# Seven seldom needed expert blocks as one loop behind one branch, in a Mamba and mixture-of-experts kernel

## Chip, core and metric

The kernel runs on one core of one Trainium2 chip. The metric is the device time of one execution in microseconds (us), the median of three runs. Engines are named as in the profile: PE (matrix products; PEld is its weight load), DVE (vector), ACT (scalar), POOL (GpSimd, which here issues the indirect DMAs) and SP (SyncE, which issues the plain DMAs).

## The reference

An input of 4096 tokens of width 256 goes through a state-space (Mamba) layer and then through a layer of eight experts, each with a residual and a LayerNorm behind it. A token is given to one expert alone, the one with the largest logit.

```python
def _L0_ffn_ref(x, Wr, br, W1, b1, W2, b2):
    D_MODEL, D_FF, N_EXP = (256, 1024, 8)
    xf = x.reshape(-1, D)
    logits = xf @ Wr.T + br
    expert_idx = jnp.argmax(logits, axis=-1)
    h = jax.nn.relu(jnp.einsum('td,efd->etf', xf, W1) + b1[:, None, :])
    y = jnp.einsum('etf,edf->etd', h, W2) + b2[:, None, :]
    out = y[expert_idx, jnp.arange(xf.shape[0])]
    return out.reshape(B, S, D)

x = L0_attn_input_tensor                      # (1, 4096, 256), float32
x = _layernorm(x + _L0_attn_ref(x, ...))      # the Mamba layer
x = _layernorm(x + _L0_ffn_ref(x, ...))       # the expert layer
```

## The kernel before

The Mamba layer works in eight blocks of 512 tokens. As soon as enough tokens have passed it, the kernel sorts them by expert and gathers them into expert blocks of 128 rows; every block has one expert. Because experts can end in blocks that are not full, up to `NSB` = 39 blocks can be needed. The first `SURE` = 32 are always computed; blocks 32 to 38, the **seldom blocks**, are needed only where the tokens are spread unluckily. A count on the chip, `total`, is loaded into a register of every engine (`held[1]`, line 1128), and a branch (`tc.If`, line 656) skips seldom blocks that are not needed. In this input none is needed: no product of a seldom block is in the trace.

**One expert block**, in the order in which PE works:

- `turn(b)` transposes the gathered rows `xg` (line 553), and DVE copies the result to `xgT` (line 564). It is issued one block ahead.
- `hidden(b, half)` makes half of the 1024 hidden columns (line 581): 16 of the 32 recorded products of a block for each half. ACT adds the bias and clips the first half (line 590), DVE the second (line 592); the result is `hT`.
- `close(b, half)` multiplies `hT` by the second weights into the accumulator `pe` (line 606).
- `finish(b)` adds up on DVE: `xs` = `xg` + b2 (line 629), `r` = `pe` + `xs` (line 631), then `layernorm` (lines 254 to 261, with one square root on ACT, line 259), which leaves `y`.
- `scatter(b)` sends `y` to its rows of the output by an indirect DMA on POOL (line 645).

Blocks 17, 20, 23, 26 and 29 are `LONG`: they hold 32 or 64 rows more, their hidden rows lie in a wider buffer (`wide`), the products of the extra rows come behind the others (line 617), and a second LayerNorm follows.

**Weights.** A block's expert weights are 128 rows of 4360 float32 values, 2.2 MB. Three buffers, `held_weights`, hold them: block b uses buffer b modulo 3. `prefetch(b)` (lines 508 to 524) gathers rows and weights up to two blocks ahead, through POOL. Where the block three before has the same expert, the load is suppressed by an index out of bounds; `same` in `table` says so, and it is set to zero where a seldom block may have overwritten the buffer.

**Order.** PE's order is the order of the program (`manual_schedule`). For the other engines a scheduler chooses the order, but nothing moves across a branch. The generator `blocks()` runs blocks 0 to 31; the first ones lie beside the Mamba layer, the last ones alone. After a block that stands in `SELDOM`, `seldom(after)` issues one branch with one or two seldom blocks in it. There are four branches: behind blocks 27 (two seldom blocks), 28 (two), 29 (one) and 31 (two). The first three follow the whole `finish` of their block. The last one precedes the `finish` of block 31. The rows of the seldom blocks are gathered into one buffer during blocks 22 to 26 (`gather_seldom`), are replaced there by the results where a block is computed, and are scattered during blocks 29 to 31 and at the end. Where the block is not needed, the indices of its scatter are out of bounds.

Of the kernel before, what the change touches and what calls it, by code (L numbers as in the profile page):

```python
# [37 lines left out]
F32 = mybir.dt.float32  # L38
# [4 lines left out]
ALU = mybir.AluOpType  # L43
# [4 lines left out]
P = 128  # L48
T, D = 4096, 256
# [30 lines left out]


SELDOM = {SURE - 5: (0, 1), SURE - 4: (2, 3), SURE - 3: (4,), SURE - 1: (5, 6)}
EPS = 1e-5
# [17 lines left out]
def mamba_moe(  # L101
# [173 lines left out]
    def order(b0, b):  # L275

        if b0 == EARLY[6] and b < SURE - b0:
            b = b % SLOTS * RUN + b // SLOTS
        return slice(b, b + 1)

    def table(b0, nb, columns, rows, early):
# [131 lines left out]
        if not early:  # L413
# [9 lines left out]

            for b in SELDOM:
                if b + SLOTS < SURE:
                    nc.vector.memset(same[:, order(b0, b + SLOTS - b0)], 0.0)
            nc.vector.scalar_tensor_tensor(eb, same, float(NE * P), eb, ALU.mult, ALU.add)
# [70 lines left out]

    xgf, openf, yf, ends_, wide_, seldom_in = {}, {}, {}, {}, {}, []
    current = 0  # L500
# [35 lines left out]
    def seldom_rows():  # L536
# [4 lines left out]
        return seldom_in[0]  # L541

    def gather_seldom(b):
        xgs[b] = ys[b] = seldom_rows()[:, (b - SURE) * D : (b - SURE + 1) * D]
        gather(xgs[b], *index[b])

# [49 lines left out]
    def close(b, half):  # L596
# [15 lines left out]
        if b in LONG:  # L612

            openf[b], n = bank("o", f"pf{b}"), more_of(b)
            for fc in range(FC):
# [4 lines left out]
                )  # L620
        if b != SURE - 1:
            finish(b)

    def finish(b):
        xg, we, py = xgs[b], wes[b], open_[b]
        xs = m2.tile([P, D], F32, tag="xs", name=f"xs{b}")

        with tc.issue_after(last[b].ins):
            nc.vector.tensor_tensor(xs, xg, we[:, OC : OC + D], ALU.add)
        r = m2.tile([P, D], F32, tag="r", name=f"r{b}")  # L630
        nc.vector.tensor_tensor(r, py[:, 0:D], xs, ALU.add)  # L631
        if b < SURE:
            ys[b] = m2.tile([P, D], F32, tag="y", name=f"y{b}")
        layernorm(m2, r, ys[b], f"m{b}")
# [17 lines left out]

    def seldom(after):

        first = SURE + SELDOM[after][0]
        with tc.If(held[1] > (first - EARLY[6]) * P, preferred_fallthrough_block=False):  # L656
            for b in (SURE + n for n in SELDOM[after]):
                wes[b] = held_weights[(after if after < SURE - 1 else after - 1) % SLOTS]
                row = nc.values_load(
                    spare[0:1, b - SURE : b - SURE + 1], engines=[mybir.EngineType.SP],  # L660
                    min_val=0, max_val=(NE - 1) * P,
                )
                nc.sync.dma_start(wes[b], experts[bass.ds(row, P), :])
                turn(b)
                for half in range(2):
                    hidden(b, half)
                for half in range(2):
                    close(b, half)

    def blocks():  # L670

        nonlocal current
        for b in range(SURE):
            current = b
            if b - 1 in SELDOM:
                seldom(b - 1)
            prefetch(b)

            for n in SELDOM.get(b + 5, ()):
                gather_seldom(SURE + n)  # L680

            if 0 < b:
                scatter(b - 1)
            for n in SELDOM.get(b - 2, ()):
                scatter(SURE + n)
            if b not in turned:
# [439 lines left out]
    for _ in quarters:  # L1126
        if current == min(SELDOM) - 3 and len(held) == 1:
            held += nc.values_load_multi_w_load_instructions(
                held[0], min_val=0, max_val=NSB * P, bass_reorder=False
            )[1]  # L1130

    seldom(SURE - 1)
    for n in SELDOM[SURE - 1]:
        scatter(SURE + n)
    finish(SURE - 1)
    scatter(SURE - 1)

# [43 lines left out]
```

## Time and profile before

| what | value |
|---|---|
| median of three runs | 494.23 us (493.94 to 494.93) |
| the profiled execution | 493.76 us |
| its span, first to last instruction | 492.1 us |
| granted PE clock, mean over the span | 0.991 |
| busy: PE, PEld, DVE, ACT, POOL | 472.7, 353.0, 346.9, 218.8, 187.3 us |
| PE's last product ends | 484.17 us |

A span is counted from the first instruction on the core to the last; the time of an execution has some 1.7 us more around it. In the profile a row of a timeline gives the start, the busy time, the engine, the line, the operation, the tiles (output, then inputs), the shapes and the number of merged instructions; in brackets stands how long the engine was idle before it and what released it. "DVEq" is the instruction queue of DVE: branches and semaphore steps, which don't count as work. Matmuls are pipelined, so their rows overlap a little, and their ends are modelled.

### The profile page before, as it was taken

The numbers are of one execution on the slowest core, as the hardware profiler recorded it, in microseconds if no ns is written. First come the engines' busy times: TensorE is split into PE (matmuls) and PEld (weight loads), VectorE is DVE, ScalarE is ACT, GpSimd is POOL, SyncE is SP. The second block draws the span as 40 slices with busy tenths as digits, with TensorE's granted clock in tenths as the row PEclk, the third lists the DMA queues.
The fourth block names the chain that finished last, engine by engine and source line by source line (L and its number), as shares of the span: only waits on it lengthen the run. The fifth ranks groups of instructions, "written<-read, shape, count | busy, mean of one in ns | idle before, by whom it ended". The sixth has DMA issues, their size and how long they took to land. (4 is left out here: it accounts for less than half of the span.)

```text
span 492.1 us, 7641 instructions
## 1 busy us (share of the span) xinstructions
PE 472.7 (96%) x2602; PEld 353.0 (72%) x2602; DVE 346.9 (71%) x1161; ACT 218.8 (44%) x452; POOL 187.3 (38%) x193
## 2 busy tenths in 40 slices
PE   8999999999999999999999999999999999998893
PEld 5344645555464675777889998999989898987782
DVE  2587979797999889869899788545565655453352
ACT  4786778777878774845342221221212121211120
POOL 2002122444447345233415242444444466542433
PEclk9999999999999999999999999999999999998997
DMA  8401012120308908506666587999871599486500
GB/s 235 156 1 44 0 44 85 45 85 1 128 1 349 361 18 277 191 2 224 218 259 254 214 296 263 375 346 367 325 300 50 202 321 318 143 293 254 194 17 23
DMA packets 23052, 89.59 MB, mean 182 GB/s; under 512 B 4898, under 2 KB 14629, under 8 KB 19298
## 3 DMA queue, kind: packets, MB, share of 16 engines
q0 software_dynamic: 8672, 74.29, 41.3%
q1 hardware_dynamic: 13378, 14.50, 9.1%
q8 instruction: 23, 0.38, 0.3%
q10 hardware_dynamic: 960, 0.27, 0.3%
q14 instruction: 19, 0.16, 0.1%
HBM read 87.35 MB, written 9.54 MB: 197 GB/s over the span
## 5 line engine op out<-in xcount | busy, mean ns | idle before, releaser
L722 PE MATMUL pm<-xTb,win 128*128 128x512 f32 (+1 forms) x260 | 120.6, 595 | 0.5 <-DMA win<-in_W_in 0.5
L581 PEld LDWEIGHTS ph<-xgT,we 128*128 128x128 f32 x864 | 102.2, 194 | 9.7 <-DVEq L656 2.7
L581 PE MATMUL ph<-xgT,we 128*128 128x128 f32 x864 | 104.9, 279 | 3.3 <-DMA out<-long,tidx 2.3
L606 PE MATMUL pe<-we,hT 128*128 128x256 f32 x432 | 99.9, 381 | 0.7 <-DVE hT L592 0.7
L606 PEld LDWEIGHTS pe<-we,hT 128*128 128x128 f32 x432 | 79.5, 190 | 11.7 <-DVE hT L592 1.5
L735 DVE SCALAR_TENSOR_TENSOR acc<-xc,cw,acc 128x512 f32<-128x512 f32 x96 | 71.2, 771 | 15.5 <-ACT acc L731 15.1
L722 PEld LDWEIGHTS pm<-xTb,win 128*128 128x128 f32 x260 | 47.3, 191 | 46.9 <-issue 40.4
L520 POOL DMA_INDIRECT we<-in_experts,widx x32 | 33.8, 1056 | 95.6 <-DVE r L631 32.3
L259 ACT ACTIVATE sdm<-sdm 128x1 f32<-128x1 f32 x32 | 6.5, 202 | 132.8 <-DVE sdm L258 132.7
L890 PE MATMUL po<-wout,sg 128*128 128x264 f32 x256 | 64.1, 392 | 0.0
L854 POOL TENSOR_TENSOR sg<-cv,sg 128x512 f32<-128x512 f32 x22 | 33.9, 1543 | 59.2 <-DVE cv L849 44.3
L890 PEld LDWEIGHTS po<-wout,sg 128*128 128x128 f32 x256 | 46.0, 190 | 10.2 <-issue 2.9
L592 DVE TENSOR_SCALAR hT<-ph,we 128x128 f32<-128x128 f32 x108 | 31.5, 343 | 29.4 <-issue 9.7
L645 POOL DMA_INDIRECT out<-y,tidx x32 | 32.9, 1028 | 42.2 <-DVE y L261 30.0
L503 POOL DMA_INDIRECT xg<-x1d,tidx x32 | 32.3, 1010 | 31.7 <-issue 6.6
L631 DVE TENSOR_TENSOR r<-pe,xs 128x256 f32<-128x256 f32 x32 | 13.5, 422 | 42.3 <-PE pe L606 38.5
L590 ACT ACTIVATE hT<-ph,we 128x128 f32<-128x128 f32 x108 | 30.8, 366 | 26.5 <-PE ph L581 18.3
L979 POOL TENSOR_SCALAR rowh<-lrow,row,code 128x256 f16<-128x256 bf16 x20 | 25.8, 1299 | 26.8 <-DVE row L971 26.8
L849 DVE SCALAR_TENSOR_TENSOR cv<-cv,dp,py 128x256 f32<-128x256 f32 x64 | 28.9, 470 | 2.4 <-PE py L842 2.4
L727 ACT ACTIVATE sg<-pm 128x512 f32<-128x512 f32 x32 | 19.0, 595 | 17.1 <-PE pm L722 14.8
L581 PE MATMUL ph<-wide,we 128*128 128x160 f32 (+1 forms) x160 | 24.4, 310 | 2.3 <-DVEq L656 2.3
L581 PEld LDWEIGHTS ph<-wide,we 128*128 128x128 f32 x160 | 23.8, 190 | 2.9 <-DVEq L656 2.7
(221 smaller groups left out, 612.3 us busy)
## 6 DMA issues: line engine op xcount, KB each, us to landing
xb<-in_x SPq DMA_DIRECT2D x8, 512.0 KB, 4.8
x1d<-x SPq DMA_DIRECT2D x8, 512.0 KB, 5.4
xTb<-in_xT SPq DMA_DIRECT2D x7, 512.0 KB, 3.5
win<-in_W_in SPq DMA_DIRECT2D x1, 512.0 KB
we<-in_W_outT SPq DMA_DIRECT2D x1, 512.0 KB
wout<-in_W_out SPq DMA_DIRECT2D x1, 512.0 KB
we<-in_experts,widx POOLq DMA_INDIRECT x32
xg<-x1d,tidx POOLq DMA_INDIRECT x32
```

What stands on the lines that cost most here:

```text
L503: nc.gpsimd.indirect_dma_start(out=to, out_offset=None, in_=x1d[0:rows, :], in_offset=bass.IndirectOffsetOnAxis(ap=at, axis=0),)
L520: nc.gpsimd.indirect_dma_start(out=wes[n][:, :], out_offset=None, in_=experts, in_offset=bass.IndirectOffsetOnAxis(ap=weights[n], axis=0), ...
L581: nc.tensor.matmul(ph[:, n * w : (n + 1) * w], lhsT=we[:, at : at + P], rhs=xgT[:, dc * w : (dc + 1) * w], start=(dc == 0), stop=(dc == DC ...
L590: nc.scalar.activation(hT[:, fc, :], ph[:, n * w : (n + 1) * w], AF.Relu, bias=bias)
L592: last[b] = nc.vector.tensor_scalar(hT[:, fc, :], ph[:, n * w : (n + 1) * w], bias, 0.0, ALU.add, ALU.max)
L606: nc.tensor.matmul(py[:, 0:D], lhsT=hT[:, fc, 0:P], rhs=out_weights(fc), start=(fc == 0), stop=(fc == FC - 1),)
L645: moved = nc.gpsimd.indirect_dma_start(out=out, out_offset=bass.IndirectOffsetOnAxis(ap=at, axis=0), in_=rows, in_offset=None, bounds_chec ...
L722: nc.tensor.matmul(pm[:, at], lhsT=win[:, dc, c * P : (c + 1) * P], rhs=xTb[:, dc, at], start=(dc == 0), stop=(dc == DC - 1),)
L735: nc.vector.scalar_tensor_tensor(acc, xc[:, c, k : k + TB], cw[:, c, k : k + 1], acc, ALU.mult, ALU.add)
L849: nc.vector.scalar_tensor_tensor(cv[:, c, at], cv[:, c, at], dp[:, c : c + 1], py[:, 0 : TB // 2], ALU.mult, ALU.add,)
L854: eng.tensor_tensor(sg[:, c, :], cv[:, c, :], sg[:, c, :], ALU.mult)
L890: nc.tensor.matmul(po[:, 0 : D + NE], lhsT=sg[:, c, j * P : (j + 1) * P], rhs=wout[:, c, :], start=(c == 0), stop=(c == CC - 1),)
```

## The change

Four branches with one or two seldom blocks each become one branch, behind the products of block 28. Inside it a loop of seven rounds (`tc.For_i`) computes one seldom block in each round: it loads the expert's weights and the block's rows by SP's queue, computes, and stores the result in place of the rows. The `finish` of block 28 comes after the branch. `xs` = `xg` + b2 moves from `finish` to the end of `close`, for every block, so that for block 28 it is ahead of the branch. The gathers of the seldom rows lie in blocks 22 to 25 and their scatters in blocks 30 and 31. One weight load (block 31's) is forced where there were two (blocks 30 and 31), and the count is loaded into the registers in block 25 rather than in block 24.

```diff
-SELDOM = {SURE - 5: (0, 1), SURE - 4: (2, 3), SURE - 3: (4,), SURE - 1: (5, 6)}
+SELDOM = SURE - 4
...
-            for b in SELDOM:
-                if b + SLOTS < SURE:
-                    nc.vector.memset(same[:, order(b0, b + SLOTS - b0)], 0.0)
+            nc.vector.memset(same[:, order(b0, SELDOM + SLOTS - b0)], 0.0)
...
-    def gather_seldom(b):
-        xgs[b] = ys[b] = seldom_rows()[:, (b - SURE) * D : (b - SURE + 1) * D]
-        gather(xgs[b], *index[b])
...
-        if b != SURE - 1:
+        xss[b] = m2.tile([P, D], F32, tag="xs", name=f"xs{b}")
+
+        with tc.issue_after(last[b].ins):
+            nc.vector.tensor_tensor(xss[b], xgs[b], we[:, OC : OC + D], ALU.add)
+        if b != SELDOM:
             finish(b)
 
     def finish(b):
-        xg, we, py = xgs[b], wes[b], open_[b]
-        xs = m2.tile([P, D], F32, tag="xs", name=f"xs{b}")
-
-        with tc.issue_after(last[b].ins):
-            nc.vector.tensor_tensor(xs, xg, we[:, OC : OC + D], ALU.add)
+        we, py, xs = wes[b], open_[b], xss[b]
         r = m2.tile([P, D], F32, tag="r", name=f"r{b}")
         nc.vector.tensor_tensor(r, py[:, 0:D], xs, ALU.add)
-        if b < SURE:
-            ys[b] = m2.tile([P, D], F32, tag="y", name=f"y{b}")
+        ys[b] = m2.tile([P, D], F32, tag="y", name=f"y{b}")
         layernorm(m2, r, ys[b], f"m{b}")
...
-    def seldom(after):
-
-        first = SURE + SELDOM[after][0]
-        with tc.If(held[1] > (first - EARLY[6]) * P, preferred_fallthrough_block=False):
-            for b in (SURE + n for n in SELDOM[after]):
-                wes[b] = held_weights[(after if after < SURE - 1 else after - 1) % SLOTS]
+    def seldom():
+
+        with tc.If(held[1] > (SURE - EARLY[6]) * P, preferred_fallthrough_block=False):
+            with tc.For_i(0, NSB - SURE) as n:
+                b = SURE
+                at = seldom_rows()[:, bass.ds(n * D, D)]
+                wes[b] = held_weights[SELDOM % SLOTS]
                 row = nc.values_load(
-                    spare[0:1, b - SURE : b - SURE + 1], engines=[mybir.EngineType.SP],
+                    spare[0:1, bass.ds(n, 1)], engines=[mybir.EngineType.SP],
                     min_val=0, max_val=(NE - 1) * P,
                 )
                 nc.sync.dma_start(wes[b], experts[bass.ds(row, P), :])
+                one = m2.tile([P, D], F32, tag="y", name="seldom_x")
+                nc.sync.dma_start(one, at)
+                xgs[b] = one
                 turn(b)
                 for half in range(2):
                     hidden(b, half)
                 for half in range(2):
                     close(b, half)
+                nc.sync.dma_start(at, ys[b])
 
     def blocks():
...
-            if b - 1 in SELDOM:
-                seldom(b - 1)
+            if b - 1 == SELDOM:
+                seldom()
+                finish(SELDOM)
             prefetch(b)
 
-            for n in SELDOM.get(b + 5, ()):
-                gather_seldom(SURE + n)
+            if SELDOM - 6 <= b < SELDOM - 2:
+                for n in range(SURE + b - SELDOM + 6, NSB, 4):
+                    gather(seldom_rows()[:, (n - SURE) * D : (n - SURE + 1) * D], *index[n])
 
             if 0 < b:
                 scatter(b - 1)
-            for n in SELDOM.get(b - 2, ()):
-                scatter(SURE + n)
+            for n in range(b + 2, NSB, 2) if b >= SURE - 2 else ():
+                ys[n] = seldom_rows()[:, (n - SURE) * D : (n - SURE + 1) * D]
+                scatter(n)
...
-        if current == min(SELDOM) - 3 and len(held) == 1:
+        if current == SELDOM - 3 and len(held) == 1:
...
-    seldom(SURE - 1)
-    for n in SELDOM[SURE - 1]:
-        scatter(SURE + n)
-    finish(SURE - 1)
     scatter(SURE - 1)
```

More of the change, by code (lines that the diff above doesn't have):

```diff
@@ L496, in mamba_moe @@
     xgs, wes, turned, hid, last, open_, ys = {}, {}, {}, {}, {}, {}, {}
-    xgf, openf, yf, ends_, wide_, seldom_in = {}, {}, {}, {}, {}, []
+    xgf, openf, yf, ends_, wide_, xss, seldom_in = {}, {}, {}, {}, {}, {}, []
     current = 0
```

## The prediction

> **What bounds the kernel now.** I read the page first, then TensorE's timeline from 434 us on, the instructions of line 656 (the `If`), the stage table, and last the timeline of all engines in the tail.
>
> ```profile
> PE 472.7 (96%) x2602; PEld 353.0 (72%) x2602; DVE 346.9 (71%) x1161; ACT 218.8 (44%) x452; POOL 187.3 (38%) x193
> ...
> PEclk9999999999999999999999999999999999998997
> ```
>
> PE works 96% of the span, so only what stops PE, or lies behind its last product, is worth time. The clock row has one low slice before the end (an 8, at 443 to 455 us). The timeline shows why both matter here:
>
> ```profile
> 435.32 3.84 PE L581 MATMUL ph<-xgT,we 128*128 128x128 f32 x32
> 439.00 0.38 PE L553 MATMUL pg<-ident,xg 128*128 128x128 f32 x2
> 439.22 3.62 PE L606 MATMUL pe<-we,hT 128*128 128x256 f32 x16
> 445.16 5.47 PE L581 MATMUL ph<-xgT,we 128*128 128x128 f32 x32 [2.33 <-DMA out<-long,tidx]
> ...
> 457.38 5.47 PE L581 MATMUL ph<-wide,we 128*128 128x192 f32 x32 [2.32 <-DVEq L656]
> ...
> 469.04 3.81 PE L581 MATMUL ph<-xgT,we 128*128 128x128 f32 x32 [0.65 <-DVE y L261]
> ```
>
> The first three lines are block 27. Blocks 28, 29 and 30 start at 445.16, 457.38 and 469.04, each just after a branch (behind blocks 27, 28 and 29), and PE stands still before them for 2.33, 2.32 and 0.65 us. The only other PE gap above 0.25 us after 415 us is 0.35 us inside block 30. The DMA named at 445.16 had nothing to give; the wait is the next line's, DVE's branch:
>
> ```profile
> 456.85 0.41 DVE L261 TENSOR_SCALAR y<-r,mvm,sdm 128x256 f32<-128x256 f32 x1
> ...
> 457.38 5.17 PEld L581 LDWEIGHTS ph<-wide,we 128*128 128x128 f32 x32 [2.73 <-DVEq L656]
> ```
>
> `y` of block 28 ends at 457.26, DVE's semaphore step of line 656 falls at 457.30, PE loads weights at 457.38. So each engine that jumps over the block first waits for its own work to end, then adds to its counter what the skipped body would have added; PE's next product waits for DVE's addition, and DVE stands behind a whole LayerNorm.
>
> ```profile
> 442.80:445.10 2.30, 0.04 (x1) 0.00 (x0) 1.77 (x6) 0.20 (x1) 0.00 (x0) 1.00 0.69 266
> 445.10:450.50 5.40, 5.34 (x33) 5.34 (x33) 0.00 (x0) 1.14 (x4) 3.02 (x3) 0.68 0.58 195
> 455.00:457.30 2.30, 0.05 (x1) 0.00 (x0) 1.76 (x6) 0.20 (x1) 0.00 (x0) 1.00 0.04 12
> ```
>
> Stage rows give length, busy time of PE, PEld, DVE, ACT, POOL, then clock, DMA share, GB/s. In the two stalls DVE alone works (1.77 us of LayerNorm). After the first one the clock is 0.68 of full, and 32 products that took 3.84 us in block 27 take 5.47 us.
>
> [...]the clock is 0.5 from 445.70 to 449.11, 3.41 us[...] 2.33 us of idleness lay in the 3.41 us before. The second stall, of equal length, [...]costs nothing more. [...]PE's second branch instruction takes 0.28 to 0.31 us in all four places[...]. [...]here it is 34 to 55 ns on four engines, 64 to 310 ns on PE.[...]
>
> **The change, part by part.**
>
> *Branch behind block 27 gone.* Block 28 can start when 27 ends, as block 27 did behind 26 (no gap at 435.3). Its weights landed by 436.9, its `xgT` was copied at 440.89. Gain 2.33 us. Without this idleness [...]the half clock goes too: 5.47 - 3.84 = 1.63 us. Bounds for that: 0 (if the timed executions have no such window[...]) to twice that (if both stalls fell so); I take 1.63.
>
> *Branch behind block 29 gone.* Gain 0.65 us. Block 29 has a second group of products (L617, 1.95 us) behind the first, so DVE's `y` was nearly done when PE came; what remained is PE's own passage: products end at 468.39, own semaphore step at 468.45, branch at 468.60 for 0.28, one more wait step at 468.94, weights at 469.01. This is my price for a branch on PE alone.
>
> *Branch behind block 28 stays, ahead of `r` and the LayerNorm.* DVE's last work before it is then `xs` (it ended near 452.7, 2.4 us ahead of PE's last product), so DVE and ACT add to their counters while PE still multiplies. PE pays its own passage: 2.32 - 0.65 = 1.67 us gained. Bounds of what is left: 0.3 us (the branch instruction alone) to 3.4 us (the join below). Late next: nothing. The LayerNorm (2.2 us from `r` to the end of `y`) now runs beside block 29's first products, whose DVE half comes only about 2.7 us after its start (half of 5.47); if it slips, some tenths on `hT`.
>
> *`xs` moved up.* One 0.41 us DVE addition per block, already issued before the branch behind 27, 28 and 29 (at 452.24 for block 28). Nothing.
>
> *The loop body.* Skipped: no product of it is in the trace, and the test is that of the first branch before. Its seven row loads and seven stores on SP's queue are skipped too; SP passed its four branches at 297.6 to 299.5 and has no work behind them until the end. Nothing.
>
> *POOL.* Seven gathers and seven scatters stay, at 1.28 us each (0.97 busy and 0.30 between); two gathers move from block 26 into 24 and 25. They can delay a weight load by 1.3 us; the load for 29, issued at 436.19, landed at 446.33, and block 29 would start at 451.7, so 5 us cover it. Block 30 need no longer reload its weights by force; that load (446.01 to 455.60) was 13 us early, so nothing. The load for 31 stands behind the branch and behind block 28's products, as before; it took 9.7 us (458.19 to 467.88) and has about 18. The scatters are now four in block 30 and three in block 31: `y` of block 30 and three take 5.1 us of the 7.0 us until the last `y`. Covered; each one past that costs 1.28.
>
> *Register loads* (0.49 to 0.56 us an engine) move one block later; PE's, at 409.30, stood beside products with no gap. *One memset* less on DVE near 298 us. Nothing.
>
> *The tail.* 484.17 to 492.1, 7.9 us:
>
> ```profile
> 485.96 0.41 DVE L261 TENSOR_SCALAR y<-r,mvm,sdm 128x256 f32<-128x256 f32 x1
> 488.20 0.98 POOL L645 DMA_INDIRECT out<-y,tidx  x1 [3.74 <-issue]
> ```
>
> The last scatter starts 1.83 us behind its `y`; for block 30 it was 0.28 us (479.35 to 479.63). The last branch had long been passed by POOL (479.5), so I can't tie the extra 1.55 us to it: bounds 1.55 gained to 1.55 lost (the same delay once more behind the four scatters before it), value 0. The 0.35 us inside block 30 likewise stays.
>
> **The sum** on the profiled execution: 2.33 + 1.63 + 1.67 + 0.65 = 6.28 us. PE would end near 477.9 and the span be 485.8 instead of 492.1; the execution's own time of 493.76 becomes 487.5. The median of the three runs is 494.23, 0.47 above it; taken from the median: **487.9 us**.
>
> **Rivals.**
>
> 1. *The clock part does not show* (no half-clock window in the timed executions, or one after the remaining branch): gain 4.65, time 489.6.[...] Against: 493.76 with such a window lies close to all three runs.
>
> 2. *The branch becomes a join.* If a loop in the skipped body makes the skipping path meet on all engines and empty the DMA queues, PE waits for what is in flight at 451: the forward weight load (issued at 443, 9.6 us) and a scatter behind it, to about 453, and two meetings like the program's end (491.27 to 492.03, 0.76 us). About 2.7 us more: 490.6, and 492.2 if that idleness halves the clock. Against: no branch of before shows a meeting.
>
> 3. *It doesn't do what it says*: `r` and LayerNorm still stand ahead of the branch on DVE. Then 2.32 stays: gain 4.61, time 489.6. The order of the code speaks against it.
>
> 4. *Slower: block 31's weights come late.* POOL's order is a scheduler's, and it now orders all after the branch at once. The load takes 9.7 us and block 31 would start at 470.7, so it hurts if issued after 461.0 and makes the kernel slower if issued after about 468.3. That needs it behind block 29's scatters (ready near 465) and the four seldom ones (5.1 us): issued at 470, landed at 480, 9.3 us of stall and 1.6 of half clock, so 499. Against: before, the load (458.19) went ahead of even block 28's scatter (459.51).
>
> **How the numbers follow.** Forecast 0.64, rival 1 0.14, rival 2 0.09, rival 3 0.06, rival 4 and its like 0.07. The range goes from 485.9 (forecast with the tail's 1.55 and the 0.35) to 491.2 (rivals 1 and 3 with a tail 1.6 longer, rival 2 at its likelier end). About 0.2%, 1 us, is what a measurement can tell from no change. Faster 0.90, within 0.03, slower 0.07.
>
> **What would show it.** In the profile after: one PE gap of some 0.65 us after block 28 and none after 27 and 29; block 28's 32 products in about 3.8 us with no low clock slice before the end; `xs` of 28 before and `r` behind DVE's only branch; seven scatters of seldom rows ahead of the last `y`; PE ending near 478. Wrong if the remaining gap exceeds 2 us, or a new gap stands before block 30 or 31.

## The result and the profile after

| what | before | after |
|---|---|---|
| median of four runs each, on one chip | 494.58 us (493.94 to 495.44) | 487.7 us (486.77 to 488.9) |
| ratio of the times | | 0.9862 [0.9836, 0.9888] |
| the profiled execution | 493.76 us | 486.77 us |
| its span | 492.1 us | 485.0 us |
| PE's last product ends | 484.17 us | 477.13 us |

The changed kernel is faster by 6.9 us, where 6.3 were forecast. Its 487.7 us lie closer to the forecast of 487.9 than the two gains do, in part because the kernel before, timed again beside it, took 0.35 us longer than in the first three runs (494.58 for 494.23). PE's busy time falls by 1.7 us (472.7 to 471.0), the others change by 1.1 us at most, and the clock row has lost its low slice in front of the last one:

```profile
PE 471.0 (97%) x2602; PEld 351.9 (73%) x2602; DVE 346.9 (72%) x1160; ACT 218.8 (45%) x452; POOL 186.9 (39%) x193
...
PEclk9999999999999999999999999999999999999998
```

The same work is done with less standing about. PE's timeline shows where (start, busy time, engine, line, operation, tiles, shapes, instructions; in brackets the idle time before it and what ended it). In this kernel L574 is `hidden`, L599 `close`, L624 the addition `r`, L260 the `y` of the LayerNorm, L617 `xs`, L637 the scatter and L647 the branch:

```profile
439.39 3.62 PE L599 MATMUL pe<-we,hT 128*128 128x256 f32 x16
442.85 3.73 PE L574 MATMUL ph<-xgT,we 128*128 128x128 f32 x32
...
451.67 5.44 PE L574 MATMUL ph<-wide,we 128*128 128x192 f32 x32 [0.66 <-DVE r L624]
...
462.59 3.84 PE L574 MATMUL ph<-xgT,we 128*128 128x128 f32 x32
...
473.51 3.62 PE L599 MATMUL pe<-we,hT 128*128 128x256 f32 x16
```

Blocks 28, 29 and 30 start at 442.85, 451.67 and 462.59. Only block 29 has a bracket, 0.66 us, and it is the only PE gap above 0.25 us after 236 us. Block 28's 32 products take 3.73 us in place of 5.47. Block 27's first product stands at 435.50 us (435.32 before), so the two traces can be compared from block start to block start:

| from | before, us | after, us | difference | which rows it is |
|---|---|---|---|---|
| block 27 to 28 | 9.84 | 7.35 | -2.49 | the gap of 2.33, and 0.16 |
| block 28 to 29 | 12.22 | 8.82 | -3.40 | products 5.47 to 3.73 (1.74), gap 2.32 to 0.66 (1.66) |
| block 29 to 30 | 11.66 | 10.92 | -0.74 | the gap of 0.65, and 0.09 |
| block 30 to 31 | 7.94 | 7.35 | -0.59 | the gap of 0.35, and 0.24 |
| block 31 to PE's end | 7.19 | 7.19 | 0 | |
| sum | 48.85 | 41.63 | -7.22 | |

The small amounts beside the gaps are overlap: in the timeline a group that follows another directly starts before the modelled end of that one (in block 27 at 439.18, where the products before it end at 435.50 + 3.84 = 439.34), and a group behind a gap doesn't. The last row of sums, **the stretch** from block 27's first product to PE's end, is what the experiments below are compared by; nothing ahead of block 27 is in it.

The instructions of the branch (count, shortest, median and longest in ns, then first and last start in us):

```profile
L647 DVEq EVENT_SEMAPHORE  x1: 21/21/21, 448.9 to 448.9; - x1
L647 PEldq EVENT_SEMAPHORE  x1: 51/51/51, 451.1 to 451.1; - x1
```

and two stage rows, up to PE's last product of block 28 and the gap behind it (length, busy PE, PEld, DVE, ACT, POOL, then clock, DMA share, GB/s):

```profile
442.85:451.01 8.16, 8.16 (x53) 6.97 (x51) 4.02 (x13) 1.35 (x5) 3.02 (x3) 1.00 0.90 340
451.01:451.67 0.66, 0.00 (x1) 0.03 (x1) 0.59 (x2) 0.00 (x0) 0.00 (x0) 1.00 0.79 320
```

In the trace's records each of these steps waits for its engine's own semaphore and then adds to it. DVE adds at 448.9, 2.1 us before PE's last product of the block. PE comes at 451.0, does its own step at 451.1 and multiplies at 451.67. The clock is full. In the gap DVE has begun `r` and the LayerNorm, which no longer stand before anything on PE. The tail is what it was: the last `y` ends at 479.34, 5.71 us before the span does.

### The profile page after: what moved, and what is told of

Same layout as the page of the kernel before. It is cut to its first block, busy times and chain, and to the rows that moved or that the text cites. A ratio compares the mean times of both kernels' runs of the same rounds, so it can differ in the third digit from the quotient of the medians.

```text
span 485.0 us, 7589 instructions
## 1 busy us (share of the span) xinstructions
PE 471.0 (97%) x2602; PEld 351.9 (73%) x2602; DVE 346.9 (72%) x1160; ACT 218.8 (45%) x452; POOL 186.9 (39%) x193
## 4 chain that ended last, share of the span: by engine, by line
PE 73%; DVE 14%; issue 6%; DMA 3%; ACT 2%; POOL 1%; POOLq 0%; SPq 0%; ACTq 0%
PE ph L574 24%; PE pe L599 22%; PE pm L722 12%; PE po L890 8%; DVE acc L735 5%; DVE cv L849 2%; PE pg L546 2%; PE px L757 2%; DMA xg<-x1d,tidx 1%; DMA win<-in_W_in 1%; PE py L842 1%; PE pf L610 1%; PE pz L990 1%; DVE nma L908 1%; PE pt L816 1%
## 5 line engine op out<-in xcount | busy, mean ns | idle before, releaser
L574 PEld LDWEIGHTS ph<-xgT,we 128*128 128x128 f32 x864 | 100.7, 192 | 6.0 <-DVE stm L253 1.2
L574 PE MATMUL ph<-xgT,we 128*128 128x128 f32 x864 | 103.2, 276 | 0.0
L599 PE MATMUL pe<-we,hT 128*128 128x256 f32 x432 | 99.4, 381 | 0.0
L599 PEld LDWEIGHTS pe<-we,hT 128*128 128x128 f32 x432 | 79.7, 190 | 10.2 <-DVE lg L931 0.3
L637 POOL DMA_INDIRECT out<-y,tidx x32 | 32.9, 1027 | 43.1 <-DVE y L260 26.8
L624 DVE TENSOR_TENSOR r<-pe,xs 128x256 f32<-128x256 f32 x32 | 13.5, 422 | 45.4 <-PE pe L599 45.2
L729 ACT COPY xc<-pm 128x512 f32<-128x512 f32 x32 | 18.6, 581 | 17.0 <-PE pm L722 16.9
L731 ACT ACTIVATE acc<-pm,cb,cw 128x512 f32<-128x512 f32 x32 | 25.1, 784 | 0.0
```

The costliest lines, as they stand in the source:

```text
L574: nc.tensor.matmul(ph[:, n * w : (n + 1) * w], lhsT=we[:, at : at + P], rhs=xgT[:, dc * w : (dc + 1) * w], start=(dc == 0), stop=(dc == DC ...
L599: nc.tensor.matmul(py[:, 0:D], lhsT=hT[:, fc, 0:P], rhs=out_weights(fc), start=(fc == 0), stop=(fc == FC - 1),)
L637: moved = nc.gpsimd.indirect_dma_start(out=out, out_offset=bass.IndirectOffsetOnAxis(ap=at, axis=0), in_=rows, in_offset=None, bounds_chec ...
```

## The experiments

They answer three questions. First, what took the stall behind block 28 from 2.32 us to 0.66: the LayerNorm's place behind the branch (the prediction's step), or the loop, whose body holds one seldom block where the old one held two? Second, is the slow block 28 of before a clock lowered by PE's idleness? Third, what is the extra delay of the last scatter, which the prediction left at nothing? In the diffs "-" and "+" are against the kernel that is named. All ratios are against the kernel before, timed on the same chip.

### four_ln_behind: the four old branches, LayerNorm behind two of them

Against the kernel before:

```diff
+        xss[b] = m2.tile([P, D], F32, tag="xs", bufs=4, name=f"xs{b}")
+
+        with tc.issue_after(last[b].ins):
+            nc.vector.tensor_tensor(xss[b], xgs[b], we[:, OC : OC + D], ALU.add)
-        if b != SURE - 1:
+        if b not in (SURE - 1, SURE - 4, SURE - 5):
             finish(b)
...
                 seldom(b - 1)
+                if b - 1 in (SURE - 4, SURE - 5):
+                    finish(b - 1)
```

> The four branches of before stay, with one or two unrolled seldom blocks each and no loop; xs is added in close, and the finish of blocks 27 and 28 comes behind their branch (xs has four buffers). Theory (PE waits at a branch for what stands ahead of it on DVE): the gaps before blocks 28 and 29 fall from 2.33 and 2.32 to about 0.65 us each, the one before block 30 stays 0.65, the half-clock window in block 28 goes (1.63). Gain 1.68 + 1.67 + 1.63 = 5.0 us against before, about 489.6. Rival (the count of branches, or the unrolled body that is jumped over, is the cost): the gaps stay near 2.3 and the time near 494.6. If a loop were cheaper to pass than an unrolled body, the gaps would be clearly longer than the 0.66 us of the changed kernel.

It took 489.77 us, ratio 0.9895 [0.9867, 0.9922]. PE's timeline at the three branches:

```profile
444.31 3.81 PE L581 MATMUL ph<-xgT,we 128*128 128x128 f32 x32 [0.76 <-DVE r L631]
...
453.28 5.44 PE L581 MATMUL ph<-wide,we 128*128 128x192 f32 x32 [0.73 <-DVE r L631]
...
465.00 3.81 PE L581 MATMUL ph<-xgT,we 128*128 128x128 f32 x32 [0.72 <-DVE long L640]
```

Moving the LayerNorm behind the branch (and `xs` forward), with bodies of two blocks, turns 2.33 and 2.32 us into 0.76 and 0.73, and the half clock is gone (3.81 us). So the LayerNorm's place is **enough** for the gain at these two branches. The stretch is 43.46 us, 1.83 more than in the changed kernel for two more branches on PE's path: 0.9 us each.

### one_ln_ahead: the loop, LayerNorm ahead of its branch again

Against the changed kernel:

```diff
-        if b != SELDOM:
-            finish(b)
+        finish(b)
...
                 seldom()
-                finish(SELDOM)
```

> The changed kernel, but the finish of block 28 stands ahead of its one branch again. Theory: the gap before block 29 goes from 0.66 to 2.3 us, so 1.65 us more than the changed kernel (about 489.4), and 1.6 more where a half-clock window follows (491.0). Rival (the place of the LayerNorm is nothing, only the three other branches counted): as the changed kernel, 487.7.

The stall did not come back. Time 488.27 us, ratio 0.986 [0.9836, 0.9885], stretch 41.63 us as with the change. Three answers of its trace together contradict the step on which the prediction rested: PE's first products of block 29, the end of block 28's LayerNorm on DVE, and the branch's steps:

```profile
454.19 5.44 PE L574 MATMUL ph<-wide,we 128*128 128x192 f32 x32 [0.66 <-DVE r L623]
```

```profile
455.32 0.41 DVE L260 TENSOR_SCALAR y<-r,mvm,sdm 128x256 f32<-128x256 f32 x1
```

```profile
L646 DVEq EVENT_SEMAPHORE  x1: 21/21/21, 455.8 to 455.8; - x1
L646 PEldq EVENT_SEMAPHORE  x1: 51/51/51, 453.6 to 453.6; - x1
```

PE starts block 29 at 454.19, 1.6 us **before** DVE's step at 455.8. Here PE does not wait for DVE's addition at all, so the LayerNorm may stand where it likes. What is left to explain the gain is the loop's body.

### one_block_bodies: the old branches with one block in each of the first two

Against the kernel before; the second seldom block of each of the first two bodies is left out, with its gather and its scatter. In the program the LayerNorms stay ahead of their branches.

```diff
-SELDOM = {SURE - 5: (0, 1), SURE - 4: (2, 3), SURE - 3: (4,), SURE - 1: (5, 6)}
+SELDOM = {SURE - 5: (0,), SURE - 4: (2,), SURE - 3: (4,), SURE - 1: (5, 6)}
```

> Before, with its four branches and its LayerNorms ahead of them, but only one seldom block in the bodies behind blocks 27 and 28 (the second one of each is left out, with its gather and scatter). Theory A (PE waits at the branch because its first product behind it goes into one of three product banks, and a body of two blocks, four half-blocks of products, has used all three, the next one being emptied by DVE; a body of one block leaves the next bank untouched): the gaps before blocks 28 and 29 fall to about 0.65 us though DVE still finishes the LayerNorm first; 5.0 us less than before, about 489.7. Theory B (PE waits for DVE's addition whatever the body holds, so only the LayerNorm's place counts): gaps 2.3 us, 494.7 as before.

The gaps before blocks 28, 29 and 30 are 0.65, 0.53 and 0.67 us. The timeline behind block 27, DVE's step of that branch, and block 29's first products:

```profile
445.20 2.02 PE L581 MATMUL ph<-xgT,we 128*128 128x128 f32 x16 [0.65 <-DVE r L631]
...
446.57 0.16 DVE L260 RECIPROCAL sdm<-sdm 128x1 f32<-128x1 f32 x1 [0.69 <-ACT sdm L259]
446.77 0.41 DVE L261 TENSOR_SCALAR y<-r,mvm,sdm 128x256 f32<-128x256 f32 x1
```

```profile
L656 DVEq EVENT_SEMAPHORE  x1: 21/21/21, 445.9 to 445.9; - x1
```

```profile
453.97 5.44 PE L581 MATMUL ph<-wide,we 128*128 128x192 f32 x32 [0.53 <-DVE r L631]
```

PE starts block 28 at 445.20, 0.7 us before DVE's step at 445.9. With one block in the body PE doesn't wait for DVE's addition, and there is no loop here. The LayerNorm's place is not quite what it was, though: its last two operations on DVE, at 446.57 and 446.77, come behind DVE's step. (So the scheduler does move work across a branch here, against what the section on the kernel before says.) For this reason PE is compared with DVE's step and not with the LayerNorm's end; one_ln_ahead and the next run have theirs wholly ahead of the branch. Yet the kernel was not faster: 495.25 us, ratio 1.0018 [1.0003, 1.0033]. PE ended 4.0 us earlier (480.14), and the span ended 1.9 us later (494.0). Where that went is the tail, taken up below.

### two_block_round: the loop with two blocks in a round

Against the changed kernel, with the LayerNorm ahead of the branch as in one_ln_ahead. Three rounds of two blocks; the seventh is left out of the loop.

```diff
-            with tc.For_i(0, NSB - SURE) as n:
-                b = SURE
-                at = seldom_rows()[:, bass.ds(n * D, D)]
+            with tc.For_i(0, (NSB - SURE) // 2) as n:
+              for b in (SURE, SURE + 1):
+                at = seldom_rows()[:, bass.ds(n * D * 2 + (b - SURE) * D, D)]
```

> The changed kernel with the LayerNorm of block 28 ahead of the branch, and two seldom blocks in each round of the loop (three rounds; the seventh block is left out). Theory A (which bank the body leaves next): a gap of about 2.3 us before block 29 where the same kernel with one block in a round had 0.66; 1.65 us more than the changed kernel, 489.4, or 491 with a half-clock window. Theory B' (behind a loop PE waits for no engine, whatever its body): 0.66 us and 487.7.

It took 491.24 us, ratio 0.9934 [0.991, 0.9958]. Block 29's first products, then stage rows of the stall behind block 28 and of what follows it:

```profile
454.22 7.09 PE L574 MATMUL ph<-wide,we 128*128 128x192 f32 x32 [2.37 <-DVEq L646]
```

```profile
451.80:454.20 2.40, 0.05 (x1) 0.01 (x1) 1.77 (x6) 0.20 (x1) 0.00 (x0) 0.99 0.60 237
454.20:459.50 5.30, 5.28 (x22) 5.30 (x23) 0.00 (x0) 1.46 (x4) 4.03 (x4) 0.68 0.33 79
```

The old picture is back in a kernel with one branch: 2.37 us in which only DVE's LayerNorm works, then a clock of 0.68. Against one_ln_ahead one thing changed, two blocks in the body instead of one (and three rounds instead of seven, of which none runs); in both traces the LayerNorm ends just ahead of DVE's step. The stretch is 44.99 us: 41.63, and 1.71 more of gap (2.37 - 0.66), and 1.65 of half clock (products of 7.09 us instead of 5.44).

### no_branch: nothing to jump over

Against the changed kernel; the seldom blocks are left out altogether, their gathers and scatters stay.

```diff
-                seldom()
                 finish(SELDOM)
```

> The changed kernel without its branch and loop: the seldom blocks are left out wholly (their gathers and scatters stay). Theory: the one gap of 0.66 us goes and nothing else, so 0.66 us less than the changed kernel, about 487.0. Rival (a branch also holds up POOL or the scheduler's order elsewhere, or the tail): 1.5 us or more less, 486.2 or below.

Time 486.96 us, ratio 0.985 [0.9827, 0.9872]. In PE's timeline block 29 follows block 28 without a bracket:

```profile
448.32 3.72 PE L599 MATMUL pe<-we,hT 128*128 128x256 f32 x16
451.88 5.36 PE L574 MATMUL ph<-wide,we 128*128 128x192 f32 x32
```

The stretch is 40.73 us. One passed branch therefore costs PE 41.63 - 40.73 = 0.90 us: the gap of 0.66, and 0.24 of overlap that the products on both sides lose. The two medians don't tell the kernels apart (their intervals overlap); the stretches do.

### xs_behind: the addition of b2 left behind the branch

Against the changed kernel:

```diff
-        xss[b] = m2.tile([P, D], F32, tag="xs", name=f"xs{b}")
-
-        with tc.issue_after(last[b].ins):
-            nc.vector.tensor_tensor(xss[b], xgs[b], we[:, OC : OC + D], ALU.add)
...
-        we, py, xs = wes[b], open_[b], xss[b]
+        we, py = wes[b], open_[b]
+        xs = xss[b] = m2.tile([P, D], F32, tag="xs", name=f"xs{b}")
+
+        with tc.issue_after(last[b].ins):
+            nc.vector.tensor_tensor(xss[b], xgs[b], we[:, OC : OC + D], ALU.add)
```

> The changed kernel with the addition of b2 (xs) back in finish, so that for block 28 it stands behind the branch. (Were the loop taken, block 28's b2 would be overwritten; it is not taken here.) Theory: DVE passes the branch about 2.5 us before block 28's products end and does xs in that time, so nothing: a gap of 0.66 us and 487.7. Rival: xs comes late and delays r and the LayerNorm by 0.4 us, with a few tenths on PE where DVE is short in block 29, 488.1.

Time 489.11 us, ratio 0.9898 [0.9867, 0.993], which overlaps the changed kernel's. The timeline of DVE:

```profile
449.90 0.42 DVE L622 TENSOR_TENSOR xs<-xg,we 128x256 f32<-128x256 f32 x1 [0.71 <-DVEq L647]
...
451.69 0.42 DVE L624 TENSOR_TENSOR r<-pe,xs 128x256 f32<-128x256 f32 x1 [1.36 <-PE pe L599]
```

Behind the branch `xs` runs at 449.90 and is done 1.4 us before `r`, which waits for PE's last product in any case. The gap stays 0.66 us and blocks 28 and 29 take the time that they take in the changed kernel. The stretch is 0.43 us longer, all of it in block 30, where signals of PE came late (last section). So the profile shows no cost of `xs` behind the branch; in the time it stays unclear. Where the loop does run, b2 of block 28 would be overwritten before this kernel adds it, which is why `xs` has to move forward when `finish` moves back.

### warm_stall and warm_ahead: is the slow block a clock lowered by idleness?

Both add 12 idle transposes to PE at the first two branches of the kernel before; in warm_stall behind `seldom(b - 1)`, in warm_ahead in front of it:

```diff
+                if b - 1 <= SURE - 4:
+                    warm = bank("tr", f"warm{b}", 2)
+                    for n in range(12):
+                        nc.tensor.transpose(warm[:, n % 4 * P : (n % 4 + 1) * P], ident, ident)
```

> Before, with 12 extra transposes on PE that depend on nothing, placed behind the branches behind blocks 27 and 28, so that PE is busy for some 1.5 us of each 2.3 us stall. Theory (the slow products of block 28 come of PE's idleness in the stall): block 28's 32 products take 3.8 us instead of 5.47, no low clock slice there, the next block starts where it did: 1.6 us less than before, about 493.0. Rival (those products are slow for another reason, weights or traffic of the DMA): 5.4 us and 494.6 as before. If the transposes stand in the way, later than 494.6.

The design of warm_stall failed: 497.98 us, ratio 1.0075 [1.0049, 1.0101]. PE's timeline at the first branch shows that the transposes waited like the products:

```profile
445.63 2.79 PE L680 MATMUL warm<-ident 128*128 128x128 f32 x12 [2.41 <-DVEq L656]
448.21 3.99 PE L581 MATMUL ph<-xgT,we 128*128 128x128 f32 x32
```

They filled no stall, they followed it. One thing can be read: now they are slow (2.79 us, where the same twelve take 1.47 in warm_ahead), and block 28's products behind them are nearly not (3.99 us). Slowness goes with the time since the stall, not with block 28's weights or data. The second kernel puts them where they need not wait:

> Before, with 12 extra transposes on PE that depend on nothing, now ahead of the branches behind blocks 27 and 28, so that PE works for about 1.4 us of each 2.3 us stall while DVE does the LayerNorm. Theory (the half clock comes of PE's idleness in the stall): the next block starts where it did (gaps of about 0.9 us), block 28's products take 3.8 us, no low clock slice behind 430 us; 1.6 us less than before, 493.1. Rival (the half clock comes of something else, or the transposes delay the block): 494.7 or more.

Time 492.79 us, ratio 0.9973 [0.9954, 0.9992], a gain of 0.4 to 2.3 us.

```profile
445.93 1.47 PE L679 MATMUL warm<-ident 128*128 128x128 f32 x12
448.42 3.84 PE L581 MATMUL ph<-xgT,we 128*128 128x128 f32 x32 [1.01 <-DMA out<-long,tidx]
```

The 12 transposes take 1.47 us ahead of the branch, the idleness behind them shrinks to 1.01 us, and block 28 starts 9.84 us behind block 27, exactly as before. Its products take 3.84 us instead of 5.47, and block 29 follows 10.59 us later instead of 12.22. With the wait on DVE unchanged and PE's idleness halved, 1.63 us are gone: that is the half clock, by itself. How the stall lies against the clock's 3.413 us lengths doesn't explain it, by an estimate from the traces: the half clock at the end of this one begins at 489.18, and twelve lengths back from it (as many as lie between the two half clocks of before, last section) a border falls at 448.22, so that without the transposes 2.1 us of idleness (446.10 to 448.22) would have lain in one length, as much as was followed by the half clock in warm_stall.

### tail_op: does POOL wait for the end, or does the scatter?

Against the changed kernel, a small copy on POOL that reads the last `y`, behind the last scatter:

```diff
     scatter(SURE - 1)
+    nc.gpsimd.tensor_copy(sr[:, 0, 0:1], ys[SURE - 1][:, 0:1])
```

> The changed kernel with one more POOL instruction, a copy of one column of the last y, behind the last scatter. Theory A (the 1.8 us between the last y and its scatter belong to whatever POOL instruction stands last in the program): the scatter starts about 0.3 us behind its y, and the time is 1.0 to 1.5 us less, about 486.4. Theory B (the delay belongs to the scatter itself or to its wait): 1.8 us as before, and 487.7 or some tenths more.

Time 486.75 us, ratio 0.9849 [0.9827, 0.987]. POOL's timeline:

```profile
482.17 0.98 POOL L637 DMA_INDIRECT out<-y,tidx  x1 [7.60 <-issue]
483.14 0.20 POOL L1132 COPY sr<-y 128x1 f32<-128x1 f32 x1
```

The scatter still starts 1.82 us behind its `y`, and the copy follows it at once. The delay belongs to the scatter and not to POOL's last instruction; the copy costs nothing that shows.

### branch_last, five_seldom and branch_last_120: the number of indirect DMAs

If the branch stood behind block 31's products, nothing on PE would lie behind it. Against the changed kernel (the seven scatters go into the branch, and the forced reload of block 31's weights goes):

```diff
-SELDOM = SURE - 4
+SELDOM = SURE - 1
...
-            nc.vector.memset(same[:, order(b0, SELDOM + SLOTS - b0)], 0.0)
...
+            for n in range(SURE, NSB):
+                ys[n] = seldom_rows()[:, (n - SURE) * D : (n - SURE + 1) * D]
+                scatter(n)
...
+    seldom()
+    finish(SELDOM)
     scatter(SURE - 1)
```

> The changed kernel with its one branch moved behind the products of block 31, and the seven scatters of seldom rows inside it, behind the loop (so they are skipped with it); block 31's finish and scatter follow; no weight load is forced. Theory (PE's own passage is all that is left of the branch, and behind the last product it costs PE nothing): no gap between blocks 27 and 31, PE ends 0.66 us sooner against block 27, 487.0. Rival (the end of the program: PE's end doesn't decide, but POOL's last scatter and POOL's closing step, which in the run with four indirect DMAs less took 10.8 us in place of 3.0): with seven indirect DMAs less the end may come up to 7 us later, 494, or not at all.

PE did what was expected, with no gap behind block 27 and a stretch of 40.73 us; the time was 493.1 us, ratio 0.9962 [0.9946, 0.9978]. As in one_block_bodies the loss is in the tail. Both kernels run fewer indirect DMAs on POOL than before. The next kernel, against the changed kernel, lowers that number and touches nothing else that runs; blocks 37 and 38 are left out of the gathers, of the loop and of the scatters:

```diff
-            with tc.For_i(0, NSB - SURE) as n:
+            with tc.For_i(0, NSB - SURE - 2) as n:
...
-                for n in range(SURE + b - SELDOM + 6, NSB, 4):
+                for n in range(SURE + b - SELDOM + 6, NSB - 2, 4):
...
-            for n in range(b + 2, NSB, 2) if b >= SURE - 2 else ():
+            for n in range(b + 2, NSB - 2, 2) if b >= SURE - 2 else ():
```

> The changed kernel with seldom blocks 37 and 38 left out: five rounds in the loop, two gathers and two scatters less, so four indirect DMAs less, as in the run with one-block bodies. Theory (POOL's closing step depends on how many indirect DMAs POOL has issued): the last scatter 0.3 us behind its y, POOL's closing step some 10.8 us, the program's end 11.4 us behind the start of that scatter, 493.5. Rival (the long closing step came of the four branches or of something else in that kernel): 1.8 us, 3.0 us, 487.7.

Four indirect DMAs less, and the kernel is slower than the changed one: 493.44 us, ratio 0.9981 [0.9959, 1.0003] where that has 0.9862, though PE's stretch is 41.63 us as with the change. The last `y`, its scatter and the closing instructions of POOL in the changed kernel, then in five_seldom:

```profile
478.93 0.41 DVE L260 TENSOR_SCALAR y<-r,mvm,sdm 128x256 f32<-128x256 f32 x1
481.16 0.99 POOL L637 DMA_INDIRECT out<-y,tidx  x1 [7.60 <-issue]
...
L1172 POOLq DRAIN  x3: 51/113/3039, 480.9 to 484.8; - x3
```

```profile
479.20 0.41 DVE L260 TENSOR_SCALAR y<-r,mvm,sdm 128x256 f32<-128x256 f32 x1
479.89 0.97 POOL L637 DMA_INDIRECT out<-y,tidx  x1 [6.04 <-DVE y L260]
...
L1172 POOLq DRAIN  x3: 51/113/10767, 479.7 to 491.0; - x3
```

POOL's closing drain takes 10.77 us instead of 3.04. The third kernel gives branch_last its number back, with seven extra gathers into columns that nothing reads:

```diff
+            if 22 <= b < 22 + NSB - SURE:
+                gather(seldom_rows()[:, (NSB - SURE) * D :], *index[SURE + b - 22])
```

> The kernel with its branch behind block 31's products and the seldom scatters inside it, with seven more gathers on POOL (the rows of the seldom blocks once more, into columns that nothing reads, one in each of blocks 22 to 28), so that POOL issues 120 indirect DMAs again. Theory (POOL's closing step depends on the number of indirect DMAs): the last scatter 1.8 us behind its y and a closing step of 3.0 us, as in the kernel before and the changed one; with no branch ahead of block 31 PE ends 0.66 us sooner against block 27, so 487.0. Rival (it depends on bytes or descriptors, or the skipped scatters disturb it): a closing step of 10 us and 493.

Time 488.14 us, ratio 0.986 [0.9824, 0.9896], and POOL's drain is short again:

```profile
L1176 POOLq DRAIN  x3: 51/113/3025, 481.1 to 484.9; - x3
```

| kernel | indirect DMAs on POOL | last scatter behind its `y`, us | closing drain, us | `y` to the end of the span, us |
|---|---|---|---|---|
| before | 120 | 1.82 | 3.02 | 5.7 |
| changed | 120 | 1.82 | 3.04 | 5.7 |
| branch_last_120 | 120 | 1.82 | 3.02 | 5.7 |
| one_block_bodies | 116 | 0.28 | 10.76 | 11.6 |
| five_seldom | 116 | 0.28 | 10.77 | 11.7 |
| branch_last | 113 | 0.28 | 10.52 | 11.4 |

With the number restored the tail is restored, whatever stands where. The version with the branch last is then not measurably faster than the changed kernel (0.986 against 0.9862), although its stretch is 0.90 us shorter; no version that clearly beats it was found.

## Why the prediction was right, point by point

**The branches behind blocks 27 and 29.** Right. Their gaps are gone, with a tenth or so more than the brackets said (2.49 for 2.33, 0.74 for 0.65). The price that the prediction gave one passed branch, 0.65 us, was too small: no_branch gives 0.90, because a gap also takes the overlap of the groups beside it.

**The half clock.** Right in size (1.63 forecast, 1.74 in the products of block 28) and in cause. Two_block_round brings it back together with the idleness, and warm_ahead takes it away with the idleness alone. Rival 1, with 4.65 us of gain, fell. But 1.63 is the price in the profiled execution, and not every execution pays it. The mean clock of the 100 executions of before that were timed beside the experiments lies between 0.985 and 0.996. An estimate from the trace: the half clock behind PE's last product (5.4 of 492.1 us) alone gives 0.9945, one window of 3.41 us more gives 0.991, as profiled. By that, the 27 executions at 0.994 or more had no such window. What the clock is worth in the median is known only as warm_ahead's 0.4 to 2.3 us.

**The branch behind block 28.** Right in size, 1.66 us for 1.67, but **not for the reason given**. The step said that PE's next product waits for DVE's addition, and that this addition comes early because `r` and the LayerNorm stand behind the branch. The runs make it a table of two causes, in the gap before block 29:

| | LayerNorm ahead | LayerNorm behind |
|---|---|---|
| two blocks in the body | 2.32 (before), 2.37 (two_block_round) | 0.73 (four_ln_behind) |
| one block in the body | 0.53 (one_block_bodies), 0.66 (one_ln_ahead) | 0.66 (changed kernel) |

(In one_block_bodies the LayerNorm is ahead only in part, as said there.) PE is held up by DVE only in the upper left case, so either edit alone takes the stall away, and the change makes both. In the changed kernel the loop's one-block body has already done it; the LayerNorm's new place adds nothing to be seen, and the moved `xs` shows no effect in the profile. That the number came out is therefore partly luck: the edit on which the prediction built would have been enough, but the stall was gone without it. The trace of before held the clue. At the branch behind block 29, with one block in its body, PE started at 469.04, and DVE's step came only then:

```profile
L656 DVEq EVENT_SEMAPHORE  x1: 21/21/21, 470.4 to 470.4; - x1
```

The prediction read that 0.65 us gap as a LayerNorm almost hidden behind the products of L617. It was a branch where PE does not wait for what DVE adds.

Why two blocks matter is argued from the code, not shown: `hidden` takes one of three rotating product banks (`bank("mm", ...)`) for each half, and ACT empties the first half's bank, DVE the second's. A body of two blocks goes once round the three banks and one further, so that the next product falls on a bank which DVE empties in the body; with one block the next bank is one that was last used ahead of the body. One run fits this: the transposes of warm_stall go to another kind of bank (`tr`, two of them, which `turn` uses and DVE empties), and behind a two-block body they waited 2.41 us for DVE too. Only the body's size was varied here, never the number of banks.

**The tail and block 30.** The value 0 for the tail was right by luck: the prediction had no cause for the delay, and by the runs it stayed because the change happens to keep all 120 indirect DMAs. The bounds of 1.55 us were narrow; with 116 or 113 the end comes 5.7 to 6.0 us later. The 0.35 us inside block 30 was counted as staying, and it went, with 0.24 of overlap. The small misses are why PE ended at 477.13 and not near 477.9: 0.59 there, 0.25 of overlap at the branches and 0.11 in block 28's products make 0.95, less 0.18 because block 27 began that much later.

**POOL.** The prediction's four scatters in block 30 and three in block 31 are the order of the code, and POOL took another. All seven went in one row behind `y` of block 28, from 454.88 to 463.51 us:

```profile
451.89 1.01 POOL L517 DMA_INDIRECT we<-in_experts,widx  x1 [4.09 <-PEq L647]
...
454.88 0.98 POOL L637 DMA_INDIRECT out<-seldom,tidx  x1 [0.30 <-issue]
...
463.81 0.97 POOL L637 DMA_INDIRECT out<-y,tidx  x1 [0.30 <-DVE long L632]
...
472.59 0.97 POOL L637 DMA_INDIRECT out<-y,tidx  x1 [5.59 <-DVE y L260]
```

The scatter of block 29's `y` follows them at 463.81, POOL is idle for 5.59 us before that of block 30's `y`, and nothing waited. Rival 4 fell, as block 31's load was issued at 451.89. (Its limit of 468.3 is 1.0 us late: 461.0 and the gain of 6.28 make 467.3.) Rival 2 (a join) fell: DVE passed at 448.9 without PE, and the gap is 0.66 us. Rival 3 fell: `r` of block 28 starts at 451.05, behind DVE's step. Its price was wrong too, for in one_ln_ahead the LayerNorm ahead of the branch costs nothing.

## What to carry to other kernels

A branch that is passed costs more than its instructions: ask which engine must make up the counter that the next product waits for, and what stands ahead of that engine's step; shorten that chain, or make the skipped body smaller, which worked here (2.37 us in two_block_round, 0.66 in one_ln_ahead; by the argument above, not shown, because the next product then falls on a bank that the body doesn't use). A stall of PE was worth its own length, the overlap at its edges (0.24 us) and, where a half clock follows it, as behind the 2.33 us ahead of block 28 and not behind the 2.32 us ahead of block 29, 1.6 to 1.7 us more; in warm_ahead 12 transposes ahead of that stall kept the clock (3.84 us for the products that took 5.47). Where an edit changes how many indirect DMAs POOL issues, compare the program's end before judging the edit.

## What the hardware showed that was not expected

**POOL's end hangs on the number of indirect DMAs.** With 120 the last scatter starts 1.82 us behind its `y` and the closing drain takes 3.0 us; with 116 or 113 the scatter starts after 0.28 us and the drain takes 10.5 to 10.8 us. The end comes 5.7 to 6.0 us later in these. That it goes with the number is shown by five_seldom and branch_last_120. What counts inside stays open, and so does whether fewer is the point: in the traces these DMAs signal their end on eight semaphores in turn (111 to 118 in the records of before), and with 120 the last one falls on the eighth, with 116 on the fourth and with 113 on the first. No run tells a smaller number from a number that isn't a multiple of eight.

**Signals of PE that come late.** In the profile of xs_behind PE's completion signals stop after the one that let `r` start at 461.46 and go on at 465.60, while its products run on. DVE waits for products that had ended at 463.3:

```profile
465.62 0.88 DVE L632 TENSOR_TENSOR long<-pf,long 64x256 f32<-64x256 f32 x2 [1.99 <-PE ph L574]
```

That cost 0.43 us in block 30. The 0.35 us of the kernel before is of the same kind (products that ended at 472.85 were signalled at 474.72). Neither is at a place that the edits touch, and the cause is open.

**The half clock of block 28 lasted 3.41 us, and PE had worked for 1.08 us of the 3.41 us ahead of it.** Stage rows of the kernel before, each of that length: ahead of and in the half clock of block 28, the two around the second stall, and ahead of and in the half clock of the tail:

```profile
442.29:445.70 3.41, 1.08 (x7) 0.68 (x6) 1.77 (x6) 0.20 (x1) 0.00 (x0) 1.00 0.70 271
445.70:449.11 3.41, 3.41 (x18) 3.41 (x17) 0.00 (x0) 0.53 (x3) 2.48 (x3) 0.50 0.47 125
452.53:455.94 3.41, 2.52 (x12) 1.89 (x10) 1.26 (x4) 0.00 (x0) 0.00 (x0) 1.00 0.44 182
455.94:459.35 3.41, 1.97 (x12) 1.98 (x13) 0.95 (x5) 0.57 (x3) 1.01 (x1) 1.00 0.02 5
483.25:486.66 3.41, 0.92 (x5) 0.46 (x3) 1.76 (x6) 0.20 (x1) 0.97 (x1) 1.00 0.04 5
486.66:490.07 3.41, 0.00 (x0) 0.00 (x0) 0.00 (x0) 0.00 (x0) 0.98 (x1) 0.50 0.10 37
```

The clock is 0.50 from 445.70 to 449.11 and again from 486.66, which is 40.96 us behind 445.70, twelve times 3.413; in warm_stall the half clock begins at 445.32 and at 458.97, 13.65 us or four times that apart. In the length ahead of the first PE works 1.08 us and stands for 2.33, in the one ahead of the second it works 0.92 and stands for 2.49. Counted in the same steps, a border falls at 455.94 in the second stall: PE stands for 0.9 us ahead of it and for 1.44 behind it, and the clock stays at 1.00. Two other places lie closer together. One is warm_stall's first stall, here as two stage rows:

```profile
441.90:445.30 3.40, 1.31 (x7) 0.81 (x5) 1.64 (x6) 0.20 (x1) 0.00 (x0) 1.00 0.87 348
445.30:448.70 3.40, 3.07 (x15) 3.10 (x16) 0.54 (x2) 0.00 (x0) 2.01 (x2) 0.50 0.36 85
```

PE works 1.31 us of the first and stands for 2.1, and the clock of the second is 0.50. The other is the end of one_block_bodies:

```profile
478.70:482.10 3.40, 1.44 (x7) 0.93 (x5) 1.82 (x7) 0.20 (x1) 1.43 (x2) 1.00 0.03 3
482.10:485.50 3.40, 0.00 (x0) 0.00 (x0) 0.25 (x1) 0.00 (x0) 0.97 (x1) 1.00 0.11 39
485.50:488.90 3.40, 0.00 (x0) 0.00 (x0) 0.00 (x0) 0.00 (x0) 0.00 (x0) 0.50 0.00 0
```

PE stands for 1.9 us of the first of these, and the clock of the next is still 1.00. From these two places it is estimated that the half clock set in here between 1.9 and 2.1 us of idleness in one length. Idleness is not all that counts, though. In no_branch the clock is 0.50 from 44.7 to 48.1 us, behind a length in which PE stood for only 0.2 us:

```profile
41.30:44.70 3.40, 3.21 (x16) 2.00 (x15) 2.96 (x6) 2.54 (x5) 0.00 (x0) 1.00 0.45 157
44.70:48.10 3.40, 3.40 (x6) 0.96 (x6) 3.40 (x6) 0.44 (x1) 2.15 (x2) 0.50 0.01 2
```

Small products (128x8 and 16x256) lie there. The same ones, from 41.77 us in the kernel before and from 42.67 in the changed kernel, were followed by a clock of 1.00; what made the difference was not tried.
